# Attention layer in written order: one whole projection piece between two groups of transposes, and a tile of sums per four heads

## Chip, cores and metric

The kernel runs on one core of one Trainium2 chip. The metric is the device time of one execution in microseconds; a run's value is the median of its executions.

## The reference, cut to what matters

Two layers on an image batch of 4 x 384 x 64 x 64 in float32. The first (a normalised scan layer) takes the first 6,860 us or so and is not touched. The second is attention over a 7 x 7 neighbourhood, 12 heads of 32 channels:

```python
qkv = einsum('oc,bchw->bohw', w_qkv, gn(x)) + b_qkv          # projections q, k, v
logits = stack([sum_c(q * k_pad[..., di:di+H, dj:dj+W]) for di, dj in 7x7]) + rel_bias
attn = softmax(logits, axis=-1)
out  = einsum('bnhwk,bnkchw->bnchw', attn, v_win)             # weighted values
x    = x + einsum('oc,bchw->bohw', w_proj, out) + b_proj      # out projection
```

## The kernel before

An image is cut into 8 stripes of 8 rows, a stripe into 4 blocks of 16 columns, and a block into 3 units of four heads: 384 units in all. One unit: four score matmuls (`scores`), bias and minimum on VectorE, exponential on ScalarE, reciprocal of the sums on VectorE and normalisation on GpSimd (`normalised`), twelve transposes with two copies `ta` on VectorE and one copy `tb` on ScalarE (`weighted`), and twelve matmuls for the weighted values (`attended`). Beside each unit the program makes one piece of a projection (three accumulated matmuls into one bank): the out projection of the last stripe, then k, v and q of the next one. In every step the scores of a unit, the normalisation of the unit before it and the transposes of the one before that stand together.

```python
ps_l = tile_pool(name="ps_l", bufs=4, space=PSUM)   # scores
ps_t = tile_pool(name="ps_t", bufs=2, space=PSUM)   # transposes
ps_v = tile_pool(name="ps_v", bufs=1, space=PSUM)   # weighted values
ps   = tile_pool(name="ps1_", bufs=1, space=PSUM)   # every projection piece
...
def scores(b, s, bl, m, blk):
    for hh in range(4):
        nc.tensor.matmul(lg[:, :NK], blk["q"][pr, m, ...], blk["k"][pr, m, ...])
        nc.vector.tensor_tensor_reduce(sg[:, hh, :], lg[:, :NK], bias[...], ...)
        act(sg[:, hh, :], sg[:, hh, :], AF.Exp, ..., accum_out=blk["sum"][:, 4*m+hh : 4*m+hh+1])
    return sg

def normalised(m, sg, blk):
    nc.vector.reciprocal(rs, blk["sum"][:, 4*m : 4*m+4])
    for hh in range(4):
        nc.gpsimd.tensor_scalar(sg[:, hh, :], sg[:, hh, :], rs[:, hh:hh+1], None, ALU.mult)
...
for m in range(NJ):                        # a unit
    sg = scores(b, s, bl, m, blk)
    if turned is not None:
        attend()                           # weighted values of an older unit
    turned = None
    if pending:
        normalised(*pending[-1][:3])       # the unit before this one
    if len(pending) > 1:
        pm, psg, pblk, *rest = pending.pop(0)
        turned = (pm, *weighted(pm, psg, pblk), pblk, *rest)   # 8 + 4 transposes
    pending.append((m, sg, blk, bl, b, s, aT))
    if ends and next(ends[0], None) is None:   # one piece of a projection
        ends.pop()
    elif not ends:
        next(ahead, None)
```

A scheduler then orders the instructions of each engine, so the order on the chip is not this one: it often put the twelve transposes round a cut piece, and in 133 of the 368 units between 6960 and 9380 us it put the reciprocal of a unit directly behind that unit's own bias steps, where it waits for the exponentials (counted in the trace).

## Time and profile before

| | before |
|---|---|
| median of 4 runs | 9406.49 us (9403.56 to 9408.85) |
| span of the profiled run | 9402.5 us |
| first scores of layer 1 start | 6861.0 us |
| TensorE after 6900 us: idle / busy | 215.1 / 2287.4 us |
| unbroken runs of score matmuls for 384 units | 489 |

"Idle" is the sum of the gaps between TensorE's matmul records, "busy" the rest, so the two add up to the length of the stage; this is used for every kernel below. The lines of the profile are in the prediction.

### The profile page before, as it was taken

To read this page: it belongs to the slowest core of one execution; us is meant where nothing else is said; L and a number is where in the kernel's file an instruction comes from. 1 tells how busy PE (TensorE), PEld (TensorE's weight loads), DVE (VectorE), ACT (ScalarE), POOL (GpSimd) and SP (SyncE) were. 2 spreads that over 40 slices of the span, in tenths; PEclk is the share of its full clock that TensorE was granted. 3 is DMA by queue.
4 is the path that set the end of the run, shared out by engine and by line. 5 is a ranking of instruction groups with operands and counts; after the bars stand their busy time and mean duration, and the time that the engine had idled before them with its cause. 6 is when DMAs were issued, how large, how long until landed. Compare 5 with 4: busy or idle time off the path is not lost. (4 is left out here: it accounts for less than half of the span.)

```text
span 9402.5 us, 141121 instructions
## 1 busy us (share of the span) xinstructions
PE 7733.7 (82%) x45882; PEld 5668.8 (60%) x45882; DVE 7512.0 (80%) x15604; ACT 5726.1 (61%) x13566; POOL 7641.1 (81%) x6679
## 2 busy tenths in 40 slices
PE   6877787778777887787778877887799999999998
PEld 5666666666666666666666666666554555555555
DVE  6888988898889888889898888888855555556555
ACT  5676666666666676666666666666544444444444
POOL 5898989888989898898889998999856666666666
PEclk8887888788888887788878887888699999999999
DMA  3111111111111111111111111111122222222222
GB/s 98 51 49 60 55 51 44 56 55 51 49 52 61 48 45 53 61 52 48 52 56 49 43 46 57 49 44 45 47 83 83 77 81 77 74 79 79 75 78 61
DMA packets 301925, 558.02 MB, mean 59 GB/s; under 512 B 61916, under 2 KB 185580, under 8 KB 301060
## 3 DMA queue, kind: packets, MB, share of 16 engines
q1 hardware_dynamic: 301188, 549.00, 18.6%
q8 instruction: 364, 5.96, 0.3%
q14 instruction: 373, 3.06, 0.1%
HBM read 446.33 MB, written 84.73 MB: 56 GB/s over the span
## 5 line engine op out<-in xcount | busy, mean ns | idle before, releaser
L96 ACT ACTIVATE da<-dt,nega 128x256 f32<-128x256 f32 x6144 | 2922.9, 477 | 1425.8 <-DVE hs L558 974.7
L538 POOL TENSOR_TENSOR db<-dtx,B 128x1024 f32<-128x1024 f32 x1536 | 3620.7, 2357 | 30.1
L558 DVE TENSOR_TENSOR_SCAN hp<-da,state,db 128x256 f32<-128x256 f32 x2880 | 2154.2, 748 | 303.7 <-POOL state L569 193.3
L558 DVE TENSOR_TENSOR_SCAN hs<-da,state,db 128x256 f32<-128x256 f32 x2880 | 2119.0, 736 | 341.8 <-ACT da L96 341.7
L909 POOL TENSOR_SCALAR sg<-sg,rsum 128x308 f32<-128x308 f32 x1536 | 1603.9, 1064 | 917.1 <-DVE rsum L907 771.1
L570 POOL TENSOR_TENSOR hs<-hs,C 128x512 f32<-128x512 f32 x1536 | 1951.8, 1271 | 123.2 <-POOL state L569 0.8
L578 PE MATMUL y<-ident,hv 128*128 128x128 f32 x6144 | 1191.1, 327 | 954.7 <-DVE hv L565 948.7
L578 PEld LDWEIGHTS y<-ident,hv 128*128 128x128 f32 x6144 | 850.1, 165 | 1396.3 <-DVE hv L565 1280.4
L96 ACT ACTIVATE sg<-sg,mx 128x308 f32<-128x308 f32 x1536 | 830.8, 542 | 872.7 <-DVE mx L894 840.4
L578 PE MATMUL y<-ident,hs 128*128 128x128 f32 x6144 | 1156.2, 321 | 141.5 <-POOL hs L570 140.1
L381 PE MATMUL mm_ps<-xn,w_in 128*128 128x256 f32 x4608 | 1162.6, 404 | 2.0 <-DVE xn L357 2.0
L565 DVE TENSOR_TENSOR hv<-hp,C 128x512 f32<-128x512 f32 x1536 | 1044.5, 680 | 0.0
L578 PEld LDWEIGHTS y<-ident,hs 128*128 128x128 f32 x6144 | 900.6, 169 | 189.4 <-POOL hs L570 186.0
L381 PEld LDWEIGHTS mm_ps<-xn,w_in 128*128 128x128 f32 x4608 | 924.3, 207 | 132.9 <-issue 3.0
L894 DVE CUSTOM_DVE_ANT_0 sg<-lg_ps,bias 128x308 f32<-128x308 f32 x1536 | 653.9, 474 | 270.4 <-PE lg_ps L888 270.0
L569 POOL COPY state<-hs 128x2 f32<-128x2 f32 x1536 | 289.1, 188 | 526.9 <-DVE hs L558 466.8
L388 PE MATMUL mm_ps<-xb,dcv 128*128 128x256 f32 x3072 | 716.5, 379 | 0.0
L388 PEld LDWEIGHTS mm_ps<-xb,dcv 128*128 128x128 f32 x3072 | 567.3, 190 | 72.3
L488 PE MATMUL mm_ps<-xd,w_dt 24*128 24x256 f32 x768 | 332.4, 573 | 293.5 <-DVE yg L605 290.6
L616 PE MATMUL mm_ps<-yg,w_out 128*128 128x256 f32 x2304 | 518.8, 379 | 0.0
L926 DVE COPY ta<-pt_ps 110x512 f32<-110x512 f32 x768 | 490.7, 680 | 33.4 <-PE pt_ps L921 28.4
L936 ACT COPY tb<-pt_ps 88x512 f32<-88x512 f32 x384 | 223.0, 581 | 426.8 <-PE pt_ps L932 422.7
(145 smaller groups left out, 10677.7 us busy)
## 6 DMA issues: line engine op xcount, KB each, us to landing
B<-bcrows SPq DMA_DIRECT2D x256, 512.0 KB
C<-bcrows SPq DMA_DIRECT2D x256, 512.0 KB
vw<-vd SPq DMA_DIRECT2D x1792, 33.0 KB
xr<-x SPq DMA_DIRECT2D x28, 1056.0 KB
vd<-v SPq DMA_DIRECT2D x280, 96.0 KB
xi<-in_x_dram SPq DMA_DIRECT2D x64, 384.0 KB
x<-xo SPq DMA_DIRECT2D x64, 384.0 KB
o<-x SPq DMA_DIRECT2D x96, 256.0 KB
```

Source lines behind the costliest of these rows:

```text
L96: ins = nc.scalar.activation(o, i, func, **kw)
L381: nc.tensor.matmul(pb[:, k, :], w_in[:, j, m * P : (m + 1) * P], xn[:, j, :], start=(j == 0), stop=(j == NJ - 1),)
L388: nc.tensor.matmul(pb[:, k, :], dcv[:, d, c, :], xb[:, d, c : c + T], start=(c == 0), stop=(c == KC - 1),)
L538: nc.gpsimd.tensor_tensor(db, h["dtx"].unsqueeze(1).broadcast_to([P, NG, T]), h["bc"][g][0], ALU.mult)
L558: nc.vector.tensor_tensor_scan(to[:, k, :], da[:, k, :], db[:, 2 * half + k, :], state[:, d, n + k : n + k + 1] if I % NCHUNK else 0.0, AL ...
L565: nc.vector.tensor_tensor(hv, hp, ct[:, 0:2, :], ALU.mult)
L570: nc.gpsimd.tensor_tensor(hs, hs, ct[:, 2:4, :], ALU.mult)
L578: nc.tensor.matmul(y[:, half, :], t[:, k, half * P : (half + 1) * P], ident, is_transpose=True, start=(first and half == 0), stop=(last an ...
L616: nc.tensor.matmul(h["po", first][:, m - first, :], w_out[:, d, m * P : (m + 1) * P], h["yg"][d], start=(d == 0), stop=(d == ND - 1),)
L894: nc.vector.tensor_tensor_reduce(sg[:, hh, :], lg[:, :NK], bias[:, 4 * m + hh, :], -1.0, BIG, ALU.add, ALU.min, mx[:, hh : hh + 1],)
L909: nc.gpsimd.tensor_scalar(sg[:, hh, :], sg[:, hh, :], rs[:, hh : hh + 1], None, ALU.mult)
L926: nc.vector.tensor_copy(t[: KN[0], :, :].rearrange("p a q -> p (a q)"), pt[: KN[0], :])
```

## The change

Its intent: in layer 1 the order of instructions on TensorE, VectorE, ScalarE and GpSimd is taken from the text, not from the scheduler, and the text is put in an order in which nothing on TensorE should wait. The twelve transposes are cut into two groups with one whole projection piece between them; the reciprocal of a unit moves ahead of the next unit's scores; each unit has its own tile of four sums, so that it does not share one with units still in work. Smaller parts: residual loads `o` for all three out pieces at once, the input load of a stripe started earlier, and the last image's statistics after the first projection.

```diff
+            es.enter_context(tc.manual_schedule(engines=in_step))
...
+                sums = w2.tile([P, 4], F32, tag="sum", name=f"sum_{b}_{s}_{bl}_{m}", bufs=4)
...
-                        accum_out=blk["sum"][:, 4 * m + hh : 4 * m + hh + 1],
+                        accum_out=sums[:, hh : hh + 1],
...
-            def weighted(m, sg, blk):
+            def turned_pair(sg, pair):      # 4 transposes + copy ta on VectorE
...
+            def turned_rest(sg):            # 4 transposes + copy tb on ScalarE
...
+            def step():
...
+                if turned is not None:
+                    attend(*turned)
...
+                if divided is not None:
+                    m, sg, *rest = divided
+                    ta = [turned_pair(sg, 0), turned_pair(sg, 1)]
+                    return lambda: (m, ta, turned_rest(sg), *rest)
...
+                for u in range(UNITS):
+                    now = divide()                     # reciprocal + normalise, previous unit
+                    sg, sums = scores(b, s, bl, m, blk)
+                    scored = (m, sg, sums, blk, bl, b, s, aT)
+                    if u == UNITS - 2:
+                        next(ahead, None)
+                    rest = step()                      # weighted values, 8 transposes
+                    if ends:
+                        ends.pop(0)()                  # one whole piece ...
...
+                    elif u == UNITS - 1:
...
+                        ahead = begun(n + 2)
...
+                    else:
+                        next(ahead, None)              # ... or one of k, v, q
+                    turned = rest()                    # 4 transposes
+                    divided = now
```

## The prediction

> **What bounds the kernel now.** I read the page's 40 slices first. The first 28 or so are layer 0; the change touches only layer 1, from about 6860 us to the end at 9402.5 us, the last 11 slices.
>
> ```profile
> PE   6877787778777887787778877887799999999998
> DVE  6888988898889888889898888888855555556555
> ACT  5676666666666676666666666666544444444444
> POOL 5898989888989898898889998999856666666666
> PEclk8887888788888887788878887888699999999999
> ```
>
> In layer 1 TensorE is the one full engine, at a full clock; VectorE and ScalarE are half used. A digit 9 hides up to a tenth, so next the busy time by windows, over four stretches of 500 us (the sum of the four):
>
> ```profile
> sum 2000.00, PE 1829.87 PEld 1007.62 DVE 1171.39 ACT 908.57 POOL 1272.42; mean PE 457.47 PEld 251.90 DVE 292.85 ACT 227.14 POOL 318.11
> ```
>
> TensorE is idle 170 us in 2000, 8.5%. The waits of TensorE between 6960 and 9380 us (who waited, on whom: us in total, times, longest) say for what:
>
> ```profile
> PE pt_ps L932 <- DVE ta L926: 174.1, 234, 1.7
> PE mm_ps L964 <- ACT sg L96: 11.1, 22, 0.5
> ```
>
> Nearly all of it is one wait: the third group of transposes waits until VectorE has copied the first one out of PSUM. The timeline of TensorE shows one unit (four heads) with a piece of the v projection, and after the dots the odd scores in units without a piece:
>
> ```profile
> 7565.01 0.81 PE L888 MATMUL lg_ps<-k,q 32*128 32x308 f32 x8
> 7565.74 0.64 PE L944 MATMUL pv_ps<-ta,vw 110*32 110x128 f32 x16
> 7566.20 0.40 PE L944 MATMUL pv_ps<-tb,vw 88*32 88x128 f32 x8
> 7566.54 1.09 PE L921 MATMUL pt_ps<-ident,sg 128*110 128x128 f32 x8
> 7567.46 0.81 PE L826 MATMUL mm_ps<-w_qkv,xn 128*128 128x384 f32 x2
> 7569.61 0.64 PE L932 MATMUL pt_ps<-ident,sg 128*88 128x128 f32 x4 [1.34 <-DVE ta L926]
> 7570.09 1.46 PE L826 MATMUL mm_ps<-w_qkv,xn 128*128 128x384 f32 x4
> ```
>
> ```profile
> 7544.75 0.79 PE L888 MATMUL lg_ps<-k,q 32*128 32x308 f32 x2
> 7545.83 0.64 PE L932 MATMUL pt_ps<-ident,sg 128*88 128x128 f32 x4 [0.29 <-DVE ta L926]
> 7546.40 0.80 PE L888 MATMUL lg_ps<-k,q 32*128 32x308 f32 x6
> ```
>
> Two things to see. Only a third of the piece (x2 of x6) stands between the two groups of transposes, too little to cover the copy. And four heads' scores (x8: two passes each) take 0.81 us, while one head's alone (x2) takes 0.79 us: scores split into one and three cost nearly twice. Why the copy is late is in VectorE's timeline of the same unit:
>
> ```profile
> 7567.43 0.08 DVE L894 DVE_READ_ACCUMULATOR2_ANT mx<- 128x1 f32 x1
> 7568.77 0.18 DVE L907 RECIPROCAL rsum<-sum 128x4 f32<-128x4 f32 x1 [1.25 <-ACT sg L96]
> 7568.87 1.29 DVE L926 COPY ta<-pt_ps 110x512 f32<-110x512 f32 x2
> ```
>
> The reciprocal stands ahead of the copies and idles 1.25 us for the exponentials of the scores just made. So the loop is scores, exponentials, reciprocal, copy, transposes: each unit's critical chain crosses four engines. All columns of a block's sums lie in one tile, which can make the reciprocal of the older unit wait for the newer one's exponentials.
>
> [...] So the order written is what a wait blocks; the trace agrees (1.34 us, with the rest of the piece standing behind it). [...]
>
> **The change part by part.** The number of matmuls, copies and DMAs is the same; only order and the sum tiles change. Comparing instruction orders, layer 0's TensorE rows are the same; layer 1 becomes strictly: scores x4, weighted values, eight transposes, one whole piece (three matmuls), four transposes. On VectorE the reciprocal of a unit now stands before the next unit's scores, with its own sums tile, and no longer between scores and copies.
>
> (a) The unit by starts of the timeline: scores 0.74, weighted 0.80, eight transposes 0.92, four transposes 0.48, sum 2.94 us. A piece: v 0.81 + 1.38 = 2.19; the out projection's x2 and x4 0.86 + 1.81 = 2.67, an unsplit q piece 2.77, so 2.70 for k, q, o.
> Does the copy now hide? From the start of scores, VectorE begins at 0.82, four reductions at 0.40 pitch end at 2.5, then perhaps block end 0.55, then the first copy, done by 3.7 at worst. The whole piece ends at 2.46 + 2.19 = 4.65 or 5.2. It hides by a microsecond.
>
> (b) New stall: the input normalisation (line 780) moves to a stripe's first unit, after the copies and just before the k piece that needs it. Copies end at 3.8, its first slice at 4.4 (three in 1.76 us), TensorE stands ready at 2.46: 1.9 us per stripe.
>
> (c) A middle stripe is twelve units, nine pieces of k, q, o and four of v: 12 x 2.94 + 9 x 2.70 + 4 x 2.19 + 1.9 = 35.3 + 24.3 + 8.8 + 1.9 = 70.3 us. Now: successive stripes' out projections start 78.1 us apart. Gain 7.8 us, of it about 5.6 idle (174 us over 31 stripes), and the rest split scores (I count 459 runs of scores for 369 units in the timeline, 90 extra at 0.75 us = 67 us, 2.2 a stripe), less the new stall.
>
> (d) The other stripes, estimated likewise. Four that prepare the last stripe of an image: fewer v and narrower k, one unit without a piece: 66. Three that prepare the next image: two more v, k in two halves through the one bank, and two pieces in one unit with a wait for the bank: 84 (now 90 to 93). The last: 52 as now; units without a piece are bounded by GpSimd, 4 x 1.04 = 4.2 us (now 4.5). Sum 23 x 70.3 + 4 x 66 + 3 x 84 + 52 = 2185 us, against 9388.5 - 6957.6 = 2431 now. Gain 246.
>
> (e) The first stripe: 97 us from first scores to its out projection now, with TensorE slowed in places; in order some 83. Gain 14. Against it, the last image's statistics now stand after the first projection instead of under the wait for weights: 6 us lost (6812 to 6818 now).
>
> 9402.5 - 246 - 14 + 6 = 9149 us of span, 9153 of time. I used typical starts; the mean ones are a little longer (scores 0.78, transposes 0.95), some of it real, and small waits will turn up. I add 22: **9175 us**, a gain of 2.5%.
>
> **The rivals.** (1) A wait takes the place of the one removed. [...] the third part's copy on ScalarE stands behind the k piece's eviction, and the weighted values need it 1.2 us after the transposes end; I get 1.06 us, so the slack is slim. If that or a late DMA cost 2 us more per stripe, 60 us go: 9235, within 2%. [...] Against: the waits on ScalarE are 11 us now. (2) GpSimd becomes the bound: its floor is 384 x 4.2 = 1613 us against 2250, and a normalisation has a whole unit's slack. Unlikely, except without pieces. (3) The idle time was only lent: TensorE's wait goes, but VectorE's in-order work gates it. VectorE needs 4 x 0.40 + 1.28 + 0.2 + 0.75 = 3.8 us a unit against 5.1 to 5.6; unlikely, and it would give 9300. (4) All goes better: no stall (b) and no added waits, 9090 to 9110.
>
> **Range and chances.** The removable time is well measured: 174 us of waits and 67 us of splits. The 2% line is 9218 us. Rival 1 reaches it, alone with (b) at twice its size. Range 9110 to 9265. Faster by over 2%: 0.78; within 2%: 0.21; slower: 0.01.
>
> **What would show it.** Right: the wait of the third transposes for the copy falls from 174 us to under 25; scores come only as x8; TensorE is busy about 96% of the middle; out projections start about 70 us apart; a gap of about 2 us before the first k piece of each stripe, released by xn. Wrong: TensorE waits for tb, for sums or for windows of v in every unit; or the copies still come late because something on VectorE waits ahead of them; or piece and transposes take longer side by side than the starts say.

## The result, and the profile after

The changed kernel takes 9134.81 us (median of 4 runs, 9132.24 to 9136.5). Its ratio to the kernel before is 0.9711, with a 95% interval of 0.9694 to 0.9728: 2.9% faster. Ratios are the mean time of one kernel's fast runs over that of the other's of the same rounds, so they are not quite the ratio of the medians that are quoted. The prediction was 9175 us in a range of 9110 to 9265. The time lies in the range, 40 us below the 9175.

The page of the changed kernel, VectorE's row of the 40 slices:

```profile
DVE  6898888898889888988988888888876666666666
```

In layer 1 it has risen from mostly five tenths to six; TensorE's row and its clock show nines as before. The windows say more. First the sum over the same four stretches of 500 us as in the prediction, then the rows of the first stretch, after and before. The figure in brackets is the count of matmul records:

```profile
sum 2000.00, PE 1921.30 PEld 1140.68 DVE 1299.66 ACT 1007.61 POOL 1443.84; mean PE 480.32 PEld 285.17 DVE 324.91 ACT 251.90 POOL 360.96
7000.00:7500.00 500.00, 479.22 (x4259) 284.04 (x4257) 322.11 (x1039) 249.80 (x777) 358.12 (x352) 0.99 0.29 86
```

```profile
7000.00:7500.00 500.00, 459.19 (x3833) 254.63 (x3833) 292.59 (x926) 225.44 (x692) 317.89 (x314) 1.00 0.28 80
```

TensorE is busy 96.1% of the middle (1921.30 of 2000), as predicted. But there is something more to see. In the first stretch it does 4259 matmuls where it did 3833, 11% more, while its busy time grew only 4%. So the gain is not only less waiting: the same matmuls also take less busy time. The waits of TensorE between 6940 and 9110 us:

```profile
PE mm_ps L794 <- DVE xn L781: 48.8, 29, 1.7
PE mm_ps L974 <- DVE aT L954: 12.9, 31, 0.4
PE pt_ps L935 <- DVE ta L926: 12.4, 15, 1.0
```

The wait for the copy `ta` (174 us in the prediction's view of before) is nearly gone, and the predicted new wait for the normalised input `xn` has come, up to 1.7 us a time. A unit with a v piece in TensorE's timeline (start, duration, what):

```profile
7252.66 0.81 PE L890 MATMUL lg_ps<-k,q 32*128 32x308 f32 x8
7253.40 0.65 PE L947 MATMUL pv_ps<-ta,vw 110*32 110x128 f32 x16
7253.86 0.40 PE L947 MATMUL pv_ps<-tb,vw 88*32 88x128 f32 x8
7254.19 1.08 PE L921 MATMUL pt_ps<-ident,sg 128*110 128x128 f32 x8
7255.12 2.10 PE L827 MATMUL mm_ps<-w_qkv,xn 128*128 128x384 f32 x6
7257.05 0.60 PE L935 MATMUL pt_ps<-ident,sg 128*88 128x128 f32 x4
7257.58 0.81 PE L890 MATMUL lg_ps<-k,q 32*128 32x308 f32 x8
```

The written order, without a gap: 4.92 us from scores to scores, where the same unit before had 1.34 us of wait in it alone. On VectorE the reciprocal hardly waits any more (once, for 0.4 us, between 6940 and 9030 us), and the copies follow the bias steps at once (one unit, its other lines left out):

```profile
7231.39 0.17 DVE L909 RECIPROCAL rsum<-sum 128x4 f32<-128x4 f32 x1
...
7233.47 1.28 DVE L926 COPY ta<-pt_ps 110x512 f32<-110x512 f32 x2
```

Where the 268 us of span went (from the timelines): the distance from first scores to first out projection fell from 97 to 80 us; the 31 distances between successive out projections from 2431 to 2171; and the first scores start 8.5 us later, at 6869.5, some 4 us of it because layer 0 ended later in this run. 17 + 260 - 8.5 = 268.5.

All outputs are right. Idle and busy time of TensorE after 6900 us for all kernels, with the time that it ran at half clock and the number of unbroken runs of scores (384 is the least):

| kernel | median us | idle | busy | at half clock | runs of scores |
|---|---|---|---|---|---|
| before | 9406.49 | 215.1 | 2287.4 | 6.8 | 489 |
| after | 9134.81 | 98.1 | 2136.4 | 20.7 | 385 |
| b1: before + own sums tile | 9410.46 | 216.6 | 2292.3 | 10.2 | 489 |
| b2: before + written order | 9529.12 | 398.8 | 2224.2 | 8.0 | 384 |
| b3: before + both | 9527.45 | 400.1 | 2226.3 | 3.4 | 384 |
| a1: after, scheduler's order | 9153.48 | 46.5 | 2204.5 | 15.3 | 456 |
| a2: after, 4 transposes ahead of the piece | 9391.24 | 295.6 | 2191.9 | 0.7 | 385 |
| a3: after, scores cut 3 + 1 | 9380.38 | 70.5 | 2399.8 | 42.4 | 766 |
| a4: after, reciprocal late | 9399.17 | 224.6 | 2275.4 | 276.6 | 385 |
| a5: after, piece cut 1 + 2 | 9187.94 | 125.1 | 2159.9 | 13.7 | 385 |
| a6: after, both a4 and a5 | 9750.97 | 575.6 | 2270.9 | 191.2 | 385 |
| a7: after, xn earlier | 9067.55 | 49.7 | 2115.6 | 0.0 | 385 |
| a8: a7 and two small steps | 9042.93 | 36.9 | 2106.7 | 0.0 | 384 |
| a9: both a4 and a7 | 9235.89 | 163.3 | 2172.2 | 54.7 | 385 |

From before to after: idle -117, busy -151, together 268.

### The profile page after: what moved, and what is told of

It reads as the page before.

```text
span 9134.5 us, 141565 instructions
## 1 busy us (share of the span) xinstructions
PE 7574.6 (83%) x45882; PEld 5681.8 (62%) x45882; DVE 7496.7 (82%) x15604; ACT 5711.1 (63%) x13566; POOL 7650.8 (84%) x6679
```

## The experiments

Two theories stood at the start. A: the shared tile of sums is what made the reciprocal, and so the copies, late; the sums tile then is the part that pays. B: what pays is the new text order, of which three parts can be tried singly: a whole piece between the transposes, scores in one run, the reciprocal early. A third question is what the written order (the scheduler turned off) is worth by itself. First the kernel before, with single parts of the change.

### b1: the sums tile alone

```diff
+                blk["sum", m] = w2.tile([P, 4], F32, tag="sum", ..., bufs=4)
-                        accum_out=blk["sum"][:, 4 * m + hh : 4 * m + hh + 1],
+                        accum_out=blk["sum", m][:, hh : hh + 1],
-                nc.vector.reciprocal(rs, blk["sum"][:, 4 * m : 4 * m + 4])
+                nc.vector.reciprocal(rs, blk["sum", m])
```

> The kernel before with one sums tile per four heads, nothing else. Theory A (a shared tile of sums makes the reciprocal of the older unit wait for the newer unit's exponentials, in two units of three): the wait of the third transposes for the copy falls from 174 us to under 90, the reciprocal no longer idles 1.25 us, time 9250 to 9340. Theory B (only the order of the matmuls matters): 9380 to 9420, wait of 150 us or more.

Measured: 9410.46 us, ratio 1.0001 (0.9986 to 1.0016). The waits of TensorE over the prediction's window:

```profile
PE pt_ps L933 <- DVE ta L927: 173.1, 233, 1.7
```

It is before's wait (174.1 us, 234 times) unchanged. Theory A falls. What makes the reciprocal late is not the tile that it reads but its place: where it is late, the scheduler's order has it right behind the four bias steps of its own unit, mostly ahead of the copies, so it waits for the exponentials of its own unit, whichever tile holds their sums. It is late in 132 of 368 units here and in 133 before. A late reciprocal stands up to 3.5 us ahead of 122 of before's 234 waits for the copy, which make 129 of the 174 us; in the other 112 the copy comes too late without it.

### b2: the written order alone

```diff
+            es.enter_context(tc.manual_schedule(engines=in_step))
             ps_l = es.enter_context(tc.tile_pool(name="ps_l", bufs=4, space=PSUM))
```

> The kernel before in its own written order on the four engines, nothing else: whole piece behind the third transposes, shared sums, reciprocal between scores and copies. Both theories: slower than before, since the copy is never covered. A: in two units of three the copies start only after the exponentials, about 1.25 us later; 9600 to 9800. B: the reciprocal does not wait, each unit loses about 1 us; 9450 to 9550.

Measured: 9529.12 us, ratio 1.0127 (1.0112 to 1.0142): 1.3% slower than before. The largest three waits (6960 to 9380 us):

```profile
PE pt_ps L933 <- DVE ta L927: 230.3, 289, 1.1
PE mm_ps L857 <- DVE q L862: 49.0, 58, 0.8
PE pt_ps L922 <- POOL sg L910: 34.9, 59, 0.6
```

In the old text all twelve transposes stand together, so the third group waits for the first copy 289 times, though no wait of the reciprocal shows on VectorE here. Scores are unbroken (384 runs), and busy time is 63 us less than before; 184 us more of idle time outweigh it. The wait for the copy is only 56 us of these 184. Most of the rest are waits that before hardly had: pieces that follow one another wait for their one bank (`q` above, and 16.9 us for `v`), the transposes wait for GpSimd (34.9), and the k piece for `xn` (25.7).

### b3: both

```diff
+            es.enter_context(tc.manual_schedule(engines=in_step))
...          (and the edit of b1)
```

> The run before this one with one sums tile per four heads. A: the reciprocal's wait goes, 9450 to 9550, at least 100 us under the run with shared sums. B: within 30 us of the run with shared sums.

Measured: 9527.45 us, ratio 1.0126 (1.0109 to 1.0142), the same as b2. The sums tile is worth nothing in this order either. From here on the changed kernel is the base, with one part of it undone at a time.

### a1: the changed text in the scheduler's order

```diff
-            es.enter_context(tc.manual_schedule(engines=in_step))
```

> The changed kernel without the written order: the scheduler orders its new text. If the sums tiles and the earlier reciprocal are most of the gain: 9150 to 9230. If the order on TensorE is (whole pieces between transposes, scores in fours): 9260 to 9400, with split scores back in the trace.

Measured: 9153.48 us, ratio 0.9728 (0.9714 to 0.9743). So the new text alone brings 254 of the 272 us, and the line that gives the change its name 19 us (0.2%). The intervals of the two ratios overlap, so these 19 us are near the limit of what the runs can tell. The time lies in the range of the first expectation, but not for its reason: the sums tiles are worth nothing in b1 and b3, and the reciprocal is mostly late here. The split scores that the second one named are back. From VectorE's waits, 6940 to 9030 us:

```profile
DVE rsum L908 <- ACT sg L96: 239.6, 198, 1.6
```

The scheduler again put the reciprocal late, 198 times, and VectorE waits for the exponentials again. Yet TensorE hardly feels it (its wait for `ta` is 10.8 us in that window), as the whole piece covers the copy, and the scheduler also moved the normalisation of the input out of the way: idle time is 46.5 us, half of that of the changed kernel. It loses this gain in busy time, 68 us more, mostly by cutting scores: 456 runs instead of 385, and by starts 52 of the 68 us. 68 - 52 of idle time leaves 16, near the 19 us measured.

### a2: the third transposes ahead of the piece

```diff
                     rest = step()
+                    ready = rest()
...
-                    turned = rest()
+                    turned = ready
```

> The changed kernel with the third transposes ahead of the piece. If the piece is what covers the copy: TensorE waits about 1 us (0.7 to 1.3) for the copy in nearly every unit, some 300 to 400 us in all, 9430 to 9540. If the copy is early enough without it, 9130 to 9200.

Measured: 9391.24 us, ratio 0.9983 (0.9968 to 0.9998): 256 of the 272 us are given back by this one move. The largest wait of TensorE (6940 to 9030 us), and one unit of the timeline:

```profile
PE pt_ps L935 <- DVE ta L926: 216.3, 315, 1.0
```

```profile
7508.30 1.08 PE L921 MATMUL pt_ps<-ident,sg 128*110 128x128 f32 x8
7510.39 0.64 PE L935 MATMUL pt_ps<-ident,sg 128*88 128x128 f32 x4 [1.01 <-DVE ta L926]
```

With two banks for transposes the third group needs the first bank back. The copy that frees it comes 1 us too late if nothing stands between. Idle time rises by 197.5 us; the loss was expected at least 39 us larger, but the wait is 0.69 us on average, not 1. Busy time rises too, by 55 us, with the same matmuls. The weight loads (PEld) stand differently in the two kernels. First in a2, where scores follow the piece; then in the changed kernel, where the last four transposes do:

```profile
7519.85 0.31 PEld L890 LDWEIGHTS lg_ps<-k,q 32*128 32x128 f32 x8 [0.76 <-issue]
```

```profile
7256.73 0.12 PEld L935 LDWEIGHTS pt_ps<-ident,sg 128*88 128x88 f32 x1
```

The load of the first transpose begins 0.32 us before that transpose (7257.05), under the piece. The load of the scores begins at 7519.85, at the very start of the scores, after 0.76 us without a load. By starts, a piece followed by transposes takes 2.58 us, one followed by scores 2.67. Whether the place of the load makes this difference was not shown. The larger part of the 55 us lies in the eight transposes: from their start to the next group's, idle time taken out, they take 1.09 us where the four follow at once and 0.96 where a piece does.

### a3: the fourth head's scores apart

```diff
-                for hh in range(4):
+                def head(hh):
...
+                for hh in range(3):
+                    head(hh)
+                return sg, sums, lambda: head(3)
```

The fourth is called after the weighted values, ahead of the transposes.

> The changed kernel with the fourth head's scores behind the weighted values: three heads together, one alone. If one head alone costs TensorE what four cost: 0.7 us more in each of 384 units, 9380 to 9430. If heads add up one by one and the four only look short, no change: 9130 to 9170.

Measured: 9380.38 us, ratio 0.9969 (0.9954 to 0.9984), 246 us more than the changed kernel. One unit:

```profile
7505.05 0.80 PE L890 MATMUL lg_ps<-k,q 32*128 32x308 f32 x6
...
7506.58 0.79 PE L890 MATMUL lg_ps<-k,q 32*128 32x308 f32 x2
```

One head takes as long as three, as expected. 246 / 384 = 0.64 us for each cut; all of it is busy time (+263), while idle time falls. This is the price that before paid 105 times (489 - 384).

### a4: the reciprocal late

```diff
-                    now = divide()
                     sg, sums = scores(b, s, bl, m, blk)
                     scored = (m, sg, sums, blk, bl, b, s, aT)
+                    now = divide()
...
-                    divided = now
+                    divided, held = held, now
```

The reciprocal now belongs to the unit just scored and stands between its bias steps and the copies, as the scheduler had it before in 133 of 368 units, but now in every unit; `held` keeps the rest of the pipeline as it was.

> The changed kernel with the reciprocal of the unit just scored between its scores and the copies, so that VectorE idles about 1.25 us for the exponentials as before. The whole piece should cover most of it: copies end near 4.6 us after the scores start, 5.1 with a block's end, against a piece that ends at 4.4 (v) or 5.0 us: 9170 to 9240. If it isn't covered: 9500 and more.

Measured: 9399.17 us, ratio 0.999 (0.9974 to 1.0007). This is a clear miss: 264 us lost, where about a hundred at most were expected, on the ground that the whole piece covers most of the late copy. VectorE does what was meant, and the waits of TensorE (6940 to 9370 us) show what was overlooked:

```profile
7507.32 0.18 DVE L909 RECIPROCAL rsum<-sum 128x4 f32<-128x4 f32 x1 [1.25 <-ACT sg L96]
```

```profile
PE mm_ps L794 <- DVE xn L781: 86.8, 30, 3.5
PE mm_ps L974 <- DVE aT L954: 55.2, 31, 1.8
PE pt_ps L935 <- DVE ta L926: 49.8, 59, 2.4
```

The 1.25 us delay not only the copies but all that stands behind them on VectorE: the normalised input for the first k piece (up to 3.5 us) and the block's copy `aT` for the out projection (1.8 us each stripe). These pieces come right after the eight transposes and have no cover. On average the wait for `xn` grows from 1.7 to 2.9 us and that for `aT` from 0.4 to 1.8. Against the changed kernel each of the three waits grows by about 40 us (38.0, 42.3 and 37.4). With small ones that is 126.5 us more idle time; the other half of the loss, 139 us, is busy time. The timeline says why (the first k piece of a stripe, and after the dots the second):

```profile
7495.13 1.11 PE L921 MATMUL pt_ps<-ident,sg 128*110 128x128 f32 x8
7498.71 4.48 PE L794 MATMUL mm_ps<-xn,w_qkv 128*128 128x512 f32 x6 [2.47 <-DVE xn L781]
...
7506.02 2.74 PE L794 MATMUL mm_ps<-xn,w_qkv 128*128 128x512 f32 x6
```

The piece takes 4.48 us where 2.74 is normal: the granted clock stands at half for 276.6 us in this kernel, against 20.7 in the changed one. After this wait of 2.47 us, by windows of 1 us, the clock is at 0.50 within half a microsecond of the wait's end and stays there for some 3.4 us; it is at 0.50 too, from 7492 to 7495 us, after a wait of 2.41 us for `ta` that ends at 7491.55. How long a wait must be for the clock to fall, no run tried. What the traces show is that a fall is not cheap: after 6900 us, each stretch at half clock that ended before the run did lasts 3.41 us or a multiple of it (143 stretches in the traces of all runs together).

### a9: the reciprocal late, with xn out of the way

To test that the gaps ahead of the k piece bring the half clock, a9 joins a4 with the edit of a7 (below), which moves the normalisation of the input one unit ahead.

```diff
 (a4, and)
+                yield                       # after the normalisation, in projected
...
             ahead = begun(1)
+            next(ahead)
...
                         ahead = begun(n + 2)
+                        next(ahead, None)
```

> Late reciprocal together with the normalisation moved out of a stripe's first unit. The late reciprocal alone cost 264 us, of it 126 us more idle TensorE and some 139 us more busy time with 277 us at half clock. If the half clock comes from the 3.5 us gap ahead of the first k piece (normalisation behind late copies): the half clock is gone (under 30 us) and 9130 to 9220. If it comes from the late reciprocal in every unit: half clock stays, 9300 and more.

Measured: 9235.89 us, ratio 0.9814 (0.9798 to 0.9831), 163 us less than a4. Half clock falls from 276.6 to 54.7 us, and busy time by 103. So most of the half clock in a4 came with the late `xn`, though not all but 30 us, as was expected. Nor does every fall follow a long wait: the kernel before was at half clock from 7519.28 us on for 6.83 us, with no wait of TensorE over 0.85 us in the ten before. What stays, 168 us over a7, is the price of the late reciprocal itself; the time lies 16 us above what was expected, as the wait for `aT` stays (55.2 us) and that for the copy grows:

```profile
PE pt_ps L936 <- DVE ta L927: 73.4, 79, 2.4
```

### a5: the piece cut round the third transposes

```diff
+            def between(j):
+                if j == 0 and waiting:
+                    got.append(waiting.pop()())     # the 4 transposes
...
                             (each piece's loop over j)
+                            between(j)
```

One matmul pair of the piece stands between the two groups of transposes, two behind, as the scheduler had it before.

> The changed kernel with one matmul of the piece ahead of the third transposes and two behind, as before. Reciprocal early, so the copy is done about when the first matmul is: a wait of 0.45 us in each unit with a block's end, and 0.1 to 0.25 us more for the cut piece: 9200 to 9270. If cutting the piece is the whole of the loss before: 9330 and more.

Measured: 9187.94 us, ratio 0.9766 (0.9752 to 0.9781): 53 us lost, a little less than expected (12 us below the range). With the reciprocal early, a third of a piece (0.86 us) nearly covers the copy; the wait for `ta` is 25.6 us in 87 times (6940 to 9030 us). Half of the loss (24 us) is busy time.

### a6: late reciprocal and cut piece together

```diff
 (a4 and a5)
```

> Late reciprocal and cut piece together. If either remedy alone covers the copy, only both losses together expose it: the wait is 1.3 to 1.9 us a unit, some 500 us in all, 9600 to 9750. If the two losses only add up: about 9300, the sum of what each of the two runs lost.

Measured: 9750.97 us, ratio 1.0361 (1.0347 to 1.0375). The loss against the changed kernel is 616 us, where a4 and a5 lose 264 + 53 = 317 singly. The time lies 1 us above the range that was expected for both losses exposing the copy together. So the two parts work together: either the early reciprocal or the whole piece hides most of the copy, and without both it lies open (6940 to 9030 us):

```profile
PE pt_ps L944 <- DVE ta L935: 291.3, 208, 2.4
```

This is before's wait (147.6 us in the same window), for before's two reasons, and twice as large. One difference shows in VectorE's order: before had the late reciprocal in 133 of 368 units, a6 has it in all of them. Before's scheduler also moved other work, scores among it, into the holes; what that is worth was not tried by itself. Of the 616 us, 134 are busy time, with 191 us at half clock (6.8 in before).

### a7: the normalised input one unit earlier

```diff
                         xn[:, j, :n, :], xr[:, j, :n, :], gm[:, j, 0:1], gm[:, j, 1:2], ...
                     )
+                yield
...
             ahead = begun(1)
+            next(ahead)
...
                         ahead = begun(n + 2)
+                        next(ahead, None)
```

The normalisation is written in the last unit of the stripe ahead, one unit before the k piece that needs it, and no longer in that unit itself.

> The changed kernel with the input normalisation at the end of the stripe before, behind the last q eviction. If the gap of 1.7 us before the first k piece was only the place of that line: 49 us less wait, 9080 to 9095. If it comes back as a later copy in the next unit: 9110 to 9135.

Measured: 9067.55 us, ratio 0.9635 (0.9621 to 0.9648), 67 us faster than the changed kernel and 12 us below the range that was expected. The wait for `xn` is gone: 48 us of idle time. The other 21 us are busy time, and here the trace has no half clock at all where the changed kernel had 20.7 us.

### a8: the best version

```diff
 (a7, and)
+            for part in group_stats(mvs[NB - 1], gms[NB - 1], ps, f"b{NB - 1}"):
+                part()                      # under the wait for w_pj, as before
             pvb = ps_t.tile([P, 512], F32, tag="pt", name="pvb")
...
-                    if ends:
+                    if ends and u != NJ - 1:    # out pieces one unit later
```

> The run before this one, and the first out projection piece one unit later (13 us of waits for the block's end), and the last image's statistics under the wait for the weights (about 6 us): 9055 to 9080. If the small waits were not on the path: as the run before this one.

Measured: 9042.93 us (5 runs, 9041.53 to 9045.3), ratio 0.9608 (0.9595 to 0.9621). It beats both kernels, by 3.9% and by 1.0%, and lies 12 us below the range that was expected; the two small steps were not tried apart. The same four windows:

```profile
sum 2000.00, PE 1976.24 PEld 1183.57 DVE 1353.58 ACT 1053.45 POOL 1494.36; mean PE 494.06 PEld 295.89 DVE 338.40 ACT 263.36 POOL 373.59
```

TensorE is busy 98.8% of the middle; the next gain in this layer has to come from fewer or cheaper matmuls.

## Why the prediction was right, and where it was off

**Bound and lever: right.** TensorE was the one full engine, and both levers named (174 us of wait for the copy, split scores) were real. a2 and a3 show each alone: 256 us for the piece between the transposes, 0.64 us for each cut of the scores.

**Step (a), that the copy hides behind the whole piece: right.** The wait fell from 174 to 12 us (under 25 was the test).

**Step (a), the cost of a piece: mis-sized.** Prediction: 2.70 us for k, q and o, and 2.19 for v, taken from cut pieces and from pieces followed by scores. Measured between the two groups of transposes: 2.58 and 1.94; the four transposes behind it 0.53 instead of 0.48. Taken together, this is 9 x (0.12 - 0.05) + 4 x (0.25 - 0.05) = 1.4 us a stripe too high. A duration was carried over to a place with other neighbours.

**Why the copy was late: right for the unit shown, too general.** The prediction took one unit with a late reciprocal for all. The trace of before has it in 133 of 368 units, ahead of 129 of the 174 us of waits (b1). The chain that it lists also crosses three engines (TensorE, ScalarE, VectorE), not four.

**Step (b), the new wait for xn: right in cause and size.** 1.9 us a stripe predicted, 1.7 measured on average, 48.8 us in 29 stripes. What was not foreseen is that such a gap can also cost clock: five of the changed kernel's thirty waits for `xn` (1.7 to 1.9 us each) are followed by half clock within 2.1 us (after one of 1.70 us it stands from 7352 to 7359 us), which makes nearly all of its 20.7 us; a7, without these waits, has none.

**Steps (c) to (e), the sum: close.** Middle stripes 70.3 predicted, 69.6 measured; all 31 distances 2185 against 2171; first stripe 83 against 80; later statistics 6 against about 4.7 us (8.5 less the 3.8 by which layer 0 ended later). The clean sum gave 9153, the chip 9135. The 22 us added on top are the larger half of the miss of 40. Small waits did turn up (13.5 us for `aT`, 15.0 for `ta`, from 6900 us on), but the cheaper pieces more than paid for them.

**The kind of gain: idle time right, busy time too small.** By the prediction 174 us of waits go and 31 x 1.9 = 59 come, so idle time should fall by 115 us; it fell by 117. For busy time only the split scores were named, 67 us; it fell by 151. By starts, the scores (359 to 271 us from 6960 us on) and the pieces (1019 to 954 us), whose gain no step named, both became cheaper. Step (c) shows the hole: its parts give 5.6 + 2.2 - 1.9 = 5.9 us a stripe, not 7.8. The 59 us left over in 31 stripes had no cause in the prediction, and about as much came from the pieces. That the total fits so well is partly luck.

**The hint on the sums tile: wrong.** "Which can make the reciprocal of the older unit wait" was a dependence that the trace didn't have: b1 and b3 show no effect. The reciprocal waited for its own unit's exponentials because of its place in the order.

**Rivals.** No wait for `tb` or windows came up, and 0.8 us for GpSimd (1, 2), and VectorE didn't gate the loop (3): it is busy 65% of the middle. The good case (4), no xn stall and no added waits at 9090 to 9110, did not happen here, but a7 and a8 reach below it once the stall is taken out. That nothing but the order could help was not shown: the pools hold 4 + 2 + 1 + 1 banks, four of them for the scores, and whether three would do, with the fourth as a third one for transposes, no run tried. Nor were the change's smaller parts, the loads above all, tried by themselves.

## What to carry to other kernels

If two users of a small set of buffers wait for one another, put independent work between them, enough to cover the wait (here it fell from 174 to 12 us), and look at everything behind a late instruction on the same engine, not only at the first thing that waits: the late reciprocal cost more through `xn`, `aT` and the clock than through the copy (in a4 38 us more wait for `xn` and 42 for `aT`, and 139 us more busy time with 276.6 us at half clock, against 37 us more wait for the copy). Time the new order with durations from the same neighbours, because a piece's cost differed here with what followed it (2.58 us ahead of transposes, 2.67 ahead of scores), and test two hiding measures together as well as singly: each may cover for the other (a4 and a5 lose 264 + 53 us singly, 616 together). A written order is worth little by itself (+1.3% on the old text, about -0.2% on the new); the text's order is what pays.
